# A graph network kernel: the steps behind the second pass's first four chunks come four to eight products later, and six constant writes move to product 20

## The chip, the cores and the metric

The kernel runs on one core of a Trainium2 chip. The metric is device microseconds of one execution, with the median of several runs. One execution was also taken by the hardware profiler; its rows are quoted below. PE is the engine of matrix products, PEld its weight loads, DVE the vector engine, ACT the scalar engine, POOL the general-purpose engine (here it issues gathers, transfers that fetch rows by a list of indices), SP the engine whose queue issues the plain loads.

## The reference

Four graph layers follow one another, each with a residual and a layernorm. `x` has 2708 rows of 128, `adj` is 2708 x 2708, all float32. The change is in the first layer and reaches into the second.

```python
def _L0_gnn_ref(x, A, W1, b1, W2, b2, sigma, k):          # sigma 1, k 4
    z = leaky_relu(_lap_mul(A, x) @ W1 + b1, 0.1)
    d2 = maximum(sq[:, None] + sq[None, :] - 2.0 * (z @ z.T), 0.0)
    S = exp(-sqrt(d2 + 1e-10) / (2.0 * sigma))
    S = where(ranks < k, S, 0.0)                          # the k largest of each row
    A2 = S + A
    return _lap_mul(A2, x) @ W2 + b2                      # d * (A2 @ (d * x))

def _L1_gnn_ref(X, A, W, a):
    XW = X @ W
    s_col, s_row = XW @ a[0, :f], XW @ a[0, f:]
    den = exp(leaky_relu(s_row[:, None] + s_col[None, :], 0.01))
    num = A @ den
    return A @ (where(num != 0, den / num, 0) @ XW)

x = layernorm(x + _L0_gnn_ref(...))
x = layernorm(x + _L1_gnn_ref(...))
...
```

## The kernel before, in words

**Tiles and chunks.** The 2708 rows are 22 tiles (T) of 128, the last one of 20 rows. The columns are cut into six chunks (C) of 512, 512, 512, 512, 384 and 276, that is of 4, 4, 4, 4, 3 and 3 tiles. A product of PE takes one tile of rows as weights and one chunk's columns of the adjacency matrix, and adds into an accumulator in PSUM (`acc`). One chunk takes 21 products, and every third chunk a few more for the tile of 20 rows.

**The second pass.** It forms A2 @ y2 of the first layer, y2 being the scaled x. `by_panels` (L189) runs over the chunks in order and, for each, over the row tiles; panels of four row tiles are loaded by SP into a ring of slots (L178). The part from S has four entries a row. The largest, the row itself, is a scaling by `own_sim` (L738), and three rows are gathered from memory by POOL (`gather_near` L727, L729) into one of nine buffers called `got`, and added by DVE with their weights (L742). `sum_near(t)` (L735) does this for one tile and leaves it in `near_sum`.

**What follows a chunk.** `end_pass2(c, acc)` (L974) is called behind a chunk's last product and registers these steps:

- `finish`: `add_near` (L744) adds the chunk's near sums to the accumulator by products with the identity (L749), and ACT copies it to `hT` (L981).
- `norm0`: the W2 product, one per tile (L789); DVE scales it and adds the residual (L794); then the layernorm: statistics on DVE (L272, L273), L255, the root on ACT (L242), its reciprocal (L243), the scaling (L277).
- `turn`: PE transposes the normalized tiles (L807), ACT copies them to `xT` (L810, three buffers).
- `find_c`: one product with the second layer's column vector (L861), ACT copies it to `c_row`, which is stored in hT's columns of that chunk (L862); DVE picks each row's own value (L866).
- `compare(t)`: DVE compares a tile's value with all values in `c_row` up to the tile (L893, L895; ties in L903) and writes a mask (four buffers). Its width grows with t.
- `times_w(c, t)`: XW of a tile (L874), copied by ACT to `xwe` (L875); `keep_xw(c)` writes the chunk's rows of it to memory, issued by POOL (L880).
- `rank_rows(t)`: ACT adds up a mask's rows (L911); `rank_columns(t)`: PE adds up its columns by t products one column wide (L916).

The last chunk has a path of its own (`n + 2` and later in `end_pass2`), which the diff doesn't touch. From it the ranks of the second layer's values are formed.

**The order.** PE, DVE and ACT run this stage in the order in which the program writes the instructions (`manual_schedule`, L1016). That order comes from the class `Due` (L31): `at(n, f, *args)` registers a step to be written when product n of the pass has been written, `tick` is called after each product and writes what is due; of two steps due at one product the one registered first comes first. So a step's number says behind how many products it stands on PE's queue, and equally where it stands on DVE's and ACT's among the other steps. The 132 products of the pass are numbered through. `sum_near(t)` is due at `near_at[t]` = 24 + 23 t // 5, so tile 0's at 24, tile 21's at 120. POOL's and SP's queues are ordered by the scheduler.

With n for the number of a chunk's `finish`, the chunks' numbers are n = 40, 59, 77, 96, 112 and 132. The W2 product comes at n + 2, the turn at n + 9, find_c at n + 11, compare of the chunk's k-th tile at n + 13 + 2k, times_w at n + 14 + 2k, rank_rows at n + 16 + 2k and rank_columns at n + 20 + 2k.

The W2 product, transposes, find_c and times_w share three small accumulators in PSUM (`mis`).

**The constants.** Ahead of the pass six DVE instructions fill `rk_f`, `fold` and `sel` (L774 to L781), which are first read behind the pass.

Of the kernel before, what the change touches and what calls it, by code (L numbers as in the profile page):

```python
# [22 lines left out]
CH = 4  # L23
MAGIC = 1.5 * 2**23
OOB = 4095
# [5 lines left out]
class Due:  # L31
# [5 lines left out]
    def at(self, n, f, *args):  # L37
        self.work.append((n, len(self.work), f, args))
        self.work.sort(key=lambda w: w[:2])
# [13 lines left out]
def kernel(  # L53
# [16 lines left out]
    nc = tc.nc  # L70
# [7 lines left out]
    C = len(starts)  # L78
# [5 lines left out]
    NCH = NB // CH  # L84
# [51 lines left out]
    ident = const.tile([P, P], F32, tag="ident", name="ident")  # L136
# [227 lines left out]
    with tc.tile_pool(name="knn", bufs=1) as knn:  # L364
# [97 lines left out]
        with (  # L462
# [5 lines left out]
            for c in range(C):  # L468
# [24 lines left out]
                ts = chunk_tiles[c]  # L493
# [180 lines left out]
        with tc.tile_pool(name="keys", bufs=3) as keys:  # L674

            for n, t in enumerate([*range(4, S), *range(4), *range(S, FULL)]):
                p = pw[t]
# [66 lines left out]
    def add_near(c, acc):  # L744
        ts = chunk_tiles[c]
        for t in ts:
            p = pw[t]
            o = t * P - starts[c]
            nc.tensor.matmul(  # L749
                acc[:, o : o + p], lhsT=near_sum[:p, t, :], rhs=ident[:p, :p], start=False, stop=(t == ts[-1])  # L750
            )
# [19 lines left out]
    spare = near.rearrange("p t k -> p (t k)")  # L771
    few_n, rk_f, neg_r = (spare[:, n * T : (n + 1) * T] for n in range(3))
    fold, sel = spare[:, 3 * T : 3 * T + 2 * NCH], spare[:, 3 * T + 2 * NCH : 3 * T + 2 * NCH + 2 * NB]
    nc.vector.memset(rk_f, float(OOB))  # L774
    nc.vector.tensor_add(fold, ident[:, : 2 * NCH], ident[:, 32 : 32 + 2 * NCH])
    for g in (64, 96):
        nc.vector.tensor_add(fold, fold, ident[:, g : g + 2 * NCH])
    nc.vector.memset(sel, 0.0)
    nc.vector.tensor_copy(
        sel.rearrange("p (a v) -> p a v", v=2 * CH)[:, :, :2], fold.rearrange("p (a v) -> p a v", v=2)  # L780
    )  # L781
    nc.vector.memset(rows_d, 0.0)
    add_bias(b2_sb)
    rk = rk_pool.tile([P, T], F32, tag="rk", name="rk")
# [181 lines left out]
    at = due.at  # L966
    near_at = [24 + (23 * t) // 5 for t in range(T)]
    for t in range(T):
        at(near_at[t], sum_near, t)

    ended = [-16]
    behind_last = []

    def end_pass2(c, acc):  # L974
        n = max(due.n + 1, near_at[chunk_tiles[c][-1]] + 3, ended[-1] + 16)
        ended.append(n)
        ts = chunk_tiles[c]

        def finish():
            add_near(c, acc)  # L980
            nc.scalar.copy(hT[:, cols[c]], acc[:, : cw[c]])  # L981

        at(n, finish)
        if c < C - 1:
            at(n + 2, norm0, ts)
            at(n + 9, turn, c)
            at(n + 11, find_c, c)
            for k, t in enumerate(ts):
                at(n + 13 + 2 * k, compare, t)
                at(n + 14 + 2 * k, times_w, c, t)  # L990
                if k == len(ts) - 1:
                    at(n + 14 + 2 * k, keep_xw, c)
                if c == C - 2 and k == len(ts) - 1:
                    behind_last.append(t)
                else:
                    at(n + 16 + 2 * k, rank_rows, t)
                if t:
                    at(n + (20 if c < C - 2 else 18) + 2 * k, rank_columns, t)
        else:
            for t in behind_last:  # L1000
                at(n + 1, rank_rows, t)
            at(n + 2, norm0, ts, True)
            at(n + 2, turn, c, True)
            at(n + 2, exp_table)
            at(n + 2, find_r)
            at(n + 3, last_stats)
            at(n + 3, last_rc)
            at(n + 3, turn_c, c)
            at(n + 3, negate_r)
            for k, t in enumerate(ts[:-1]):  # L1010
                at(n + 4 + k, compare, t)
                at(n + 4 + k, rank_rows, t)
                at(n + 5 + k, rank_columns, t)
            at(n + 3 + len(ts), compare_few)
            at(n + 4 + len(ts), exp_r)

    with tc.manual_schedule(engines={nc.tensor.engine, nc.vector.engine, nc.scalar.engine}):
        by_panels(
            rows_of(y2), end_pass2, due.tick, ready, [*range(S - 4), *range(S, T - 2), *range(S - 4, S), T - 2]
        )  # L1020
        due.flush()
# [23 lines left out]
    with tc.tile_pool(name="rank", bufs=1) as rank:  # L1045
# [326 lines left out]
        for c in range(C):  # L1372
            w = cw[c]
            begins = c % GROUPS == 0
            for i0 in range(0, FULL - 1, 4):
                if i0 < S:
                    n = c * G + i0 // 4
# [389 lines left out]
```

## Time and profile before

| what | value |
|---|---|
| runs of the kernel before | 1094.03, 1094.39, 1097.14 us; median 1094.39 us |
| the profiled execution | 1093.01 us, of which the span of the profile is 1091.3 us |
| PE, weight loads | busy 1000.2 us (92%), 482.7 us (44%) |
| DVE, ACT, POOL | busy 638.5 us (59%), 336.6 us (31%), 265.2 us (24%) |
| second pass | from 290 to 443 us of the span |
| gathers of near rows (L729) | 66 on POOL, 1.063 us each; POOL idle 37.5 us before them, most of it waiting for DVE's L742 |
| masks, sums of their rows | ACT's L911 takes 1.60 us for tile 12, 2.24 us for tile 18 |

The profile is one execution on the core. The page gives busy time and idle time of each engine, and what ended an idle time (the releaser, `<-`). "remote" or "another core or an unknown queue" stands where no instruction of this core's records explains the end of a wait, "issue" where the engine waited for nothing that is shown. In a timeline row the columns are the start, the duration, the engine, the line of the program, the operation, what is written from what, the shapes, how many instructions the row joins, and in square brackets the idle time before it with its releaser. In the row `PEclk` each digit is the clock that PE was granted in one of 40 slices, in tenths of full speed, a 9 being 0.9 or more.

### The profile page before, as it was taken

Reading aid. Unit: us, or ns where it says so; the run is one execution under the profiler, and the core shown is the slowest. Engines: PE = TensorE matmul, PEld = TensorE weight load, DVE = VectorE, ACT = ScalarE, POOL = GpSimd, SP = SyncE. Lnnn points to the kernel's source line nnn. Section 1 sums busy time; section 2 is a strip of 40 time slices with the busy share of each in tenths; the row PEclk is TensorE's granted clock in tenths of the full one; section 3 lists DMA queues with packets and bytes.
Section 4 is the critical chain, followed back from the end, with each engine's and each line's share of the span. In section 5 each row is a group of like instructions: output and inputs, shape, how many; then the busy total and the mean of one; then the engine's idle time right before and its main releaser. Section 6 shows DMA issues by size and latency. Waiting matters only on the chain.

```text
span 1091.3 us, 11487 instructions
## 1 busy us (share of the span) xinstructions
PE 1000.2 (92%) x3697; PEld 482.7 (44%) x3697; DVE 638.5 (59%) x1363; ACT 336.6 (31%) x617; POOL 265.2 (24%) x339
## 2 busy tenths in 40 slices
PE   0898999999987898798799999999999999999996
PEld 0445544444433455543233333334444644565444
DVE  5885448999934477772499999998112112132122
ACT  0000126555401144612467776665001100011000
POOL 4000000000575463015584344430112100000000
PEclk9889999999997899798899999999999999999998
DMA  9999340000383556497545545555775865574752
GB/s 341 357 329 276 102 137 1 0 1 1 100 279 89 186 160 205 141 369 228 136 131 153 154 122 166 143 143 181 230 232 157 275 229 183 170 238 158 240 158 77
DMA packets 109380, 190.31 MB, mean 174 GB/s; under 512 B 13666, under 2 KB 46706, under 8 KB 109310
## 3 DMA queue, kind: packets, MB, share of 16 engines
q1 hardware_dynamic: 91408, 151.79, 42.7%
q0 software_dynamic: 17728, 37.62, 12.5%
q8 instruction: 31, 0.51, 0.2%
q14 instruction: 39, 0.32, 0.1%
q10 hardware_dynamic: 174, 0.08, 0.0%
HBM read 214.37 MB, written 4.16 MB: 200 GB/s over the span
## 4 chain that ended last, share of the span: by engine, by line
PE 66%; DVE 16%; DMA 6%; issue 4%; ACT 3%; another core or an unknown queue 2%; POOL 2%; SPq 1%; POOLq 0%; DVEq 0%; ACTq 0%
PE acc L204 31%; PE num L1571 9%; PE hacc L1428 9%; PE acc L428 7%; DVE where L702 6%; DVE near L701 5%; DMA res<-in_adjT 3%; PE acc L1322 2%; PE mis L285 1%; PE acc L699 1%; DMA part<-in_adjT 1%; DMA got<-y_rows,where 1%; ACT junk L911 1%; DVE both L483 1%
## 5 line engine op out<-in xcount | busy, mean ns | idle before, releaser
L1449 POOL DMA_INDIRECT ring<-in_adjT,slot_i x88 | 95.4, 1084 | 117.7 <-PE num L1571 88.8
L1571 PE MATMUL num<-ring,lw 128*64 128x512 f32 (+1 forms) x528 | 115.6, 560 | 3.3 <-DVE err L1413 1.4
L1428 PE MATMUL hacc<-inv,xws 128*128 128x512 f32 (+1 forms) x264 | 111.7, 559 | 0.6 <-issue 0.3
L699 PE MATMUL acc<-zT,z 128*128 128x512 f32 (+2 forms) x252 | 102.2, 552 | 0.0
L1403 ACT ACTIVATE inv<-num,plain 128x1024 f32<-128x1024 f32 x88 | 80.6, 916 | 60.9 <-PE num L1571 38.6
L253 POOL TENSOR_TENSOR rstd<-rstd,minus_half 128x4 f32<-128x4 f32 (+1 forms) x18 | 17.3, 961 | 313.4 <-DVE rstd L252 313.4
L234 ACT COPY gb<-acc 128x512 f32<-128x512 f32 (+2 forms) x18 | 9.6, 535 | 251.1 <-PE acc L204 251.1
L1413 DVE TENSOR_TENSOR err<-inv,num 128x1024 f32<-128x1024 f32 x88 | 74.4, 854 | 20.4 <-ACT inv L1406 17.6
L700 ACT COPY key<-acc 128x512 f32<-128x512 f32 (+2 forms) x126 | 67.1, 535 | 55.1 <-issue 27.9
L204 PE MATMUL acc<-ring,y 128*128 128x512 f32 (+2 forms) x192 | 81.8, 556 | 0.5 <-issue 0.5
L1428 PEld LDWEIGHTS hacc<-inv,xws 128*128 128x128 f32 x264 | 46.5, 189 | 77.6 <-issue 45.2
L729 POOL DMA_INDIRECT got<-y_rows,where x66 | 70.2, 1063 | 37.5 <-DVE near_sum L742 18.9
L204 PE MATMUL acc<-ring,xs 128*128 128x512 f32 (+2 forms) x192 | 77.9, 549 | 0.0
L1420 DVE SCALAR_TENSOR_TENSOR inv<-gb,g_inv,inv 128x1024 f32<-128x1024 f32 x88 | 77.0, 913 | 0.1
L204 PE MATMUL acc<-ring,carry 128*128 128x512 f32 (+2 forms) x192 | 74.5, 542 | 0.0
L204 PE MATMUL acc<-ring,m_rows 128*128 128x512 f32 (+2 forms) x192 | 74.3, 542 | 0.0
L1417 DVE SCALAR_TENSOR_TENSOR inv<-err,inv 128x1024 f32<-128x1024 f32 x88 | 72.4, 861 | 0.1
L1406 ACT ACTIVATE inv<-inv 128x1024 f32<-128x1024 f32 x88 | 67.6, 768 | 2.8
L699 PEld LDWEIGHTS acc<-zT,z 128*128 128x128 f32 x252 | 45.8, 190 | 50.4 <-issue 45.0
L575 POOL TENSOR_TENSOR slot_e<-near,sim 128x44 f32<-128x44 f32 (+2 forms) x3 | 0.7, 245 | 269.7 <-DVE d2inv L603 267.6
L1571 PEld LDWEIGHTS num<-ring,lw 128*64 128x64 f32 x528 | 36.2, 138 | 65.0 <-issue 46.7
L701 DVE MAX8 near<-key 128x8 f32<-128x2708 f32 x21 | 62.2, 2964 | 2.7 <-ACT key L700 2.7
(378 smaller groups left out, 1392.0 us busy)
## 6 DMA issues: line engine op xcount, KB each, us to landing
ring<-in_adjT SPq DMA_DIRECT2D x86, 1024.0 KB
ring<-in_adjT SPq DMA_DIRECT2D x19, 768.0 KB
part<-in_adjT SPq DMA_DIRECT2D x12, 1024.0 KB
ring<-in_adjT SPq DMA_DIRECT2D x19, 552.0 KB
res<-in_adjT SPq DMA_DIRECT2D x4, 1280.0 KB
more<-in_adjT SPq DMA_DIRECT2D x4, 1024.0 KB
part<-in_adjT SPq DMA_DIRECT2D x3, 768.0 KB
part<-in_adjT SPq DMA_DIRECT2D x3, 552.0 KB
```

What stands on the lines that cost most here:

```text
L204: nc.tensor.matmul(accs[c][: lhsT.shape[-1], :w], lhsT=lhsT, rhs=src, start=start, stop=stop)
L428: nc.tensor.matmul(accs[c][:, : cw[c]], lhsT=y[:, i, :], rhs=src[:, : cw[c]], start=first, stop=last)
L699: nc.tensor.matmul(pks[c][:p, : cw[c]], lhsT=z2[:, :p], rhs=zT[:, cs], start=False, stop=True)
L701: nc.vector.max(near[:p, t, :], key[:p])
L729: nc.gpsimd.indirect_dma_start(out=got[:p, :], out_offset=None, in_=y2_rows[:, :], in_offset=bass.IndirectOffsetOnAxis(ap=where[:p, t, k : ...
L1403: nc.scalar.activation(inv, num[:, :w], AF.Ln, scale=plain[:, 0:1], bias=plain[:, 1:2])
L1413: nc.vector.tensor_mul(err, inv, num[:, :w])
L1417: nc.vector.scalar_tensor_tensor(inv, err, 2.0, inv, op0=ALU.subtract, op1=ALU.mult)
L1420: nc.vector.scalar_tensor_tensor(inv, gb[:, col : col + w], g_inv[:, q : q + 1], inv, op0=ALU.max, op1=ALU.mult)
L1428: nc.tensor.matmul(haccs[:, o:e], lhsT=xws[:, q, :], rhs=inv[:, o:e], start=(q == 0), stop=(q == NQ - 1))
L1449: nc.gpsimd.indirect_dma_start(out=rows[i][:KC, n, :], out_offset=None, in_=adj_half[:, :], in_offset=bass.IndirectOffsetOnAxis(ap=slot_i[ ...
L1571: nc.tensor.matmul(num[n * (BJ + 2) : (n + 1) * (BJ + 2), o:e], lhsT=lw[:, 2 * q + n, :], rhs=rows[i][:, n, c0 + o : c0 + e], start=True, ...
```

## The change

The six DVE instructions that fill `rk_f`, `fold` and `sel` become a function, registered for product 20 of the pass.

For chunks 0 to 3 (`c < C - 2`) `far` is 8, for chunk 4 it is 0. With it

- the W2 product with its layernorm moves from n + 2 to n + 6,
- the turn from n + 9 to n + 15,
- find_c from n + 11 to n + 19,
- compare, times_w, keep_xw, rank_rows and rank_columns each by eight products.

`finish` stays, so do all steps of chunks 4 and 5 and the near sums. The numbers of the W2 products are then 46, 65, 83, 102 and 114 (before 42, 61, 79, 98, 114), of the turns 55, 74, 92, 111 and 121 (before 49, 68, 86, 105, 121), of find_c 59, 78, 96, 115 and 123 (before 51, 70, 88, 107, 123).

```diff
-    nc.vector.memset(rk_f, float(OOB))
-    nc.vector.tensor_add(fold, ident[:, : 2 * NCH], ident[:, 32 : 32 + 2 * NCH])
-    for g in (64, 96):
-        nc.vector.tensor_add(fold, fold, ident[:, g : g + 2 * NCH])
-    nc.vector.memset(sel, 0.0)
-    nc.vector.tensor_copy(
-        sel.rearrange("p (a v) -> p a v", v=2 * CH)[:, :, :2], fold.rearrange("p (a v) -> p a v", v=2)
-    )
...
+    def set_constants():
...
+    at(20, set_constants)
...
         if c < C - 1:
-            at(n + 2, norm0, ts)
-            at(n + 9, turn, c)
-            at(n + 11, find_c, c)
+            far = (c < C - 2) * 8
+            at(n + (6 if far else 2), norm0, ts)
+            at(n + (15 if far else 9), turn, c)
+            at(n + (19 if far else 11), find_c, c)
             for k, t in enumerate(ts):
-                at(n + 13 + 2 * k, compare, t)
-                at(n + 14 + 2 * k, times_w, c, t)
+                at(n + far + 13 + 2 * k, compare, t)
+                at(n + far + 14 + 2 * k, times_w, c, t)
                 if k == len(ts) - 1:
-                    at(n + 14 + 2 * k, keep_xw, c)
+                    at(n + far + 14 + 2 * k, keep_xw, c)
                 if c == C - 2 and k == len(ts) - 1:
                     behind_last.append(t)
                 else:
-                    at(n + 16 + 2 * k, rank_rows, t)
+                    at(n + far + 16 + 2 * k, rank_rows, t)
                 if t:
-                    at(n + (20 if c < C - 2 else 18) + 2 * k, rank_columns, t)
+                    at(n + far + (20 if far else 18) + 2 * k, rank_columns, t)
```

The body of `set_constants` is the six instructions as they were.

More of the change, by code (lines that the diff above doesn't have):

```diff
@@ L969 @@
         at(near_at[t], sum_near, t)
+    def set_constants():
+        nc.vector.memset(rk_f, float(OOB))
+        nc.vector.tensor_add(fold, ident[:, : 2 * NCH], ident[:, 32 : 32 + 2 * NCH])
+        for g in (64, 96):
+            nc.vector.tensor_add(fold, fold, ident[:, g : g + 2 * NCH])
+        nc.vector.memset(sel, 0.0)
+        nc.vector.tensor_copy(
+            sel.rearrange("p (a v) -> p a v", v=2 * CH)[:, :, :2], fold.rearrange("p (a v) -> p a v", v=2)
+        )
+    at(20, set_constants)
     ended = [-16]
```

## The prediction

> **What bounds the kernel now.** I read first the busy shares in 40 slices, because they tell which engine fills the stage that the change touches. The second pass runs from 290 to 443 us of the span, slices 11 to 17 of 27.3 us each.
>
> ```profile
> PE   0898999999987898798799999999999999999996
> PEclk9889999999997899798899999999999999999998
> PE 66%; DVE 16%; DMA 6%; issue 4%; ACT 3%; another core or an unknown queue 2%; POOL 2%; SPq 1%; POOLq 0%; DVEq 0%; ACTq 0%
> ```
>
> PE is the bound in nearly every slice. The slices with 7 and 8 in the PE row carry a lower granted clock as well: here PE waits, and what follows a wait is slow. The third line is the chain of waits; its 2% without a known releaser matters below.
>
> Next the waits of 286 to 460 us (who waited, for whom; total, times, longest), for the gaps of PE and what DVE and ACT met at the same time.
>
> ```profile
> PE mis L807 <- DVE xs L277: 5.8, 1, 5.8
> PE acc L749 <- issue: 5.2, 1, 5.2
> PE mis L789 <- ACT hT L981: 4.9, 3, 3.7
> PE mis L861 <- issue: 2.0, 1, 2.0
> DVE xs L794 <- remote: 10.5, 1, 10.5
> ACT hT L981 <- remote: 2.7, 1, 2.7
> ```
>
> Two gaps belong to steps that move: 5.8 us where the turn (L807) waits for the normalized rows, 3.7 where the W2 product (L789) waits for hT. The 5.2 us before L749 wait for tile 3's gathers and don't move. Last the timeline (start, duration, idle before) tells why the rows were late.
>
> ```profile
> 332.84 1.25 PE L789 MATMUL mis<-w,hT 128*128 128x128 f32 x8
> 336.51 3.60 PE L204 MATMUL acc<-ring,y 128*128 128x512 f32 x8
> 345.90 1.24 PE L807 MATMUL mis<-ident,xs 128*128 128x128 f32 x4 [5.79 <-DVE xs L277]
> 346.93 3.57 PE L204 MATMUL acc<-ring,y 128*128 128x512 f32 x4
> ```
> ```profile
> 342.08 1.12 DVE L794 SCALAR_TENSOR_TENSOR xs<-mis,d2inv,xs 128x128 f32<-128x128 f32 x4 [10.47 <-remote]
> ```
> ```profile
> 338.46 1.01 POOL L729 DMA_INDIRECT got<-y_rows,where  x1 [0.30 <-issue]
> 347.46 1.01 POOL L729 DMA_INDIRECT got<-y_rows,where  x1 [7.99 <-DVE near_sum L742]
> ```
>
> Chunk 0's W2 ends at 332.84 + 1.25 = 334.1, yet DVE, idle since 331.6, starts on it only at 342.08, 8 us late; at most other places the consumer follows PE within 0.05 us. POOL issued gathers every 1.31 us until 339.47, and DVE started 2.6 us after that. I find the same at 363.1, the end of a run of 12 gathers (ACT's copy of chunk 1 starts at 364.76 for a product that ended at 359.79), and at 421.8, after 9. Runs of three to six gathers show none. My reading is that PE's completions reach the others late at the end of long runs of gathers, until the run ends. The mechanism is not shown.
>
> **The change part by part.** Base is the profiled execution, 1093.01 us (span 1091.3 and 1.7 around it); the median of the three runs is 1094.39, 1.4 above.
>
> Constants. Six DVE instructions leave the front of the pass for product 20. DVE runs in program order, and at product 20 nothing else has been written for it since; they stay between the last search and the first sums of gathered rows. Only L738's 0.2 us passes them: 0 to -0.2, I take -0.2.
>
> A, chunk 0's turn. W2 goes from product 42 to 46, the turn from 49 to 55, so six more products stand before the turn. A 512-wide product takes 0.86 us in unbroken stretches. PE's last product before the gap ended at 345.90 - 5.79 = 340.11; six more reach 345.26, and xs is ready at 345.84 if DVE still starts at 342.08. W2 then ends at 337.5, inside the late stretch as before, whose gathers don't move: DVE holds the same sums ahead of W2's result. Idle falls from 5.79 to 0.6: -5.15. After the old gap PE ran at half rate (transposes 1.24 against 0.60 at 412.95, four half products 3.57 against 1.88): 2.3 us that end too. Sum -7.45. If instead the delay of 8 us follows the product, DVE starts at 345.5 and the turn, due at 345.3, waits 4.0: then only -1.8. If no delay comes, all of 5.79 + 2.3 = -8.1.
>
> B, chunk 1's W2, product 61 to 65: four more products (3.44 us) in an idle of 3.67, and the half rate behind it (W2 2.08 against 1.05, the next product records 1.92 and 2.83 against 1.02 and 1.96: 2.8 us) may not come.
>
> ```profile
> 365.39 2.08 PE L789 MATMUL mis<-w,hT 128*128 128x128 f32 x8 [3.67 <-ACT hT L981]
> 387.74 1.05 PE L789 MATMUL mis<-w,hT 128*128 128x128 f32 x8
> ```
>
> Bounds -6.2 and 0. But sum_near(9) now precedes chunk 1's result on DVE, find_c and compare of chunk 0 sit later, and DVE frees the nine gather buffers earlier: the program puts 39 gathers ahead of the first keep_xw on POOL's queue, not 36. The run that begins at 347.5 can grow beyond 12, and a result can be late again. I take the middle, -3.2.
>
> C, chunk 2. Nothing waits there now: the W2 at 387.74 takes 1.05 at full clock. A new late stretch costs up to the worst gap seen, 5.8, and some half rate: bounds 0 and +6.5. Nearest are the runs of three to six gathers around it, with no delay: I take a quarter, +1.6.
>
> D, chunk 3's find_c goes from product 107 to 115, with it the idle of 2.01. The run of nine gathers whose end made it late stays and meets something else: 0 to -2.0, I take 0. E: its product (0.86) and one times_w (0.22) pass from ahead of chunk 4's finish to behind it: -1.1, if the end is set as below.
>
> F, the tail. Here the delay has no cover left. Chunk 4 keeps its distances, so chunk 3's eight-later work runs into it. In the trace ACT fills the end, with rank_rows one after another.
>
> ```profile
> 423.29 1.60 ACT L911 ACTIVATE junk<-mask 128x1664 bf16<-128x1664 bf16 x1
> 441.83 0.39 ACT L981 COPY hT<-acc 128x276 f32<-128x276 f32 x1
> ```
>
> Chunk 4's finish is at 421.08. Tile 12's rank_rows begins 2.2 us behind it, and the last hT copy ends 21.1 behind it (442.22). After the change chunk 4's W2 result (product 114) stands on DVE ahead of chunk 3's find_c (115) and masks (117 on): W2 ready 3.3 us after finish, norm0 3.6 (425.25 to 428.86), own 0.85, a sum_near 1.35, tile 12's mask 1.0: 10.1 us. From there ACT has six rank_rows with their reads (1.60 + 1.68 + 1.80 + 1.91 + 2.02 + 2.12 + 0.6 = 11.7), xT and a row copy (0.95), xwe copies (0.95) and hT's 0.39: 14.0. The last copy ends 24.1 behind finish, +3.0. Bounds: 0, if ACT interleaves as well as now, and +5.9, if all of the 7.9 later start but D's 2.0 stays.
>
> Sum: -0.2 - 7.45 - 3.2 + 1.6 + 0 - 1.1 + 3.0 = -7.35. Behind the pass the next stage waits on PE, DVE and ACT and not on a transfer, so a gain is kept. 1094.4 - 7.3 = 1087.0.
>
> A rule to weigh: the Trainium skill, "Perfetto Trace Analysis", "Optimization Strategy", says to find a gap, determine what blocks, and make the dependency start sooner or end faster. This change starts it later; by that rule each chunk would lose its four products, 3.44 us. The trace sides with the rule only in the tail, since in chunks 0 and 1 PE's time is what runs out.
>
> **The rivals.** R1, slower: new late stretches. For it: DVE frees buffers sooner, gather runs grow, and every run over eight had a late result at its end. Against: runs behind 365 had three to six gathers, DVE-bound. It decides when two of the results of chunks 1 to 3 are over 3.44 us late beyond what four products hide: each a gap and half rate of 6 us. -0.2 - 7.45 + 0 + 2 x 6 - 1.1 + 3.0 = +6.2, 1100.6.
>
> R2, no change: the delay follows the product. A gives -1.8, B 0, C 0, E -1.1, tail +3.0, constants -0.2: -0.1, 1094.3. For it: only one delay of 8 us was seen, and 334.1 + 8 fits as well as the end of the gathers. Against: the 2.6 us from the end of the run to the consumer come back as 1.6 and 0.9 at the two other places.
>
> R3, more: late results nowhere on PE's path. A -8.1, B -6.2, C 0, D -2.0, E -1.1, tail +3.0, constants -0.2: -14.6, 1079.8.
>
> That the change does nothing is true of the constants alone: 0.2 us at most.
>
> **How the numbers follow.** The forecast 1087.0 and its near neighbours 0.40, R3 and what lies towards it 0.16, R2 0.18, R1 0.26. Of a time, 0.3% (3.3 us) is about what a measurement of this kernel can tell from no change. The first two are faster: 0.56; R2 mostly within: 0.17; R1 and a little of R2 slower: 0.27. The forecast's own range is 1083 to 1091 (A's and B's bounds); the range of 8 in 10 takes in R3 and most of R1: 1079 to 1099.
>
> **What would show it.** A: chunk 0's turn with under 1 us idle before it, DVE's L794 twin still starting near 342, PE's clock at 1.0 from 340 to 362. B and C: idle before chunk 1's and 2's W2 and turn; a gap over 3 us speaks for R1, and then POOL's gathers must show a run over eight that ends 1 to 3 us before the late consumer. F: tile 12's rank_rows 10 us behind chunk 4's finish, the last hT copy 24 behind it. I am wrong if DVE starts on chunk 0's result about 8 us after W2's new end (R2), or if PE's gaps in the pass are no smaller in sum.

## The result, and the profile after

The changed kernel takes 1092.95 us (median of 11 runs, 1090.33 to 1098.79) against 1094.03 us before (11 runs, 1088.47 to 1097.14). The ratio is 0.9999 with an interval of 0.9977 to 1.0021: no change that the measurement can tell. The forecast was 1087.0 us and faster. The profiled execution has a span of 1091.3 us, the same as before.

Behind L774 the lines of the changed kernel are shifted: L794 is now L786, L789 is L781, L807 is L799, L911 is L903, L981 is L985, L916 is L908. First the page of the changed kernel: PE's busy tenths and granted clock.

```profile
PE   0898999999989897798699999999999999999996
PEclk9889999999999899698899999999999999999998
```

Slice 13 (327 to 355 us) rose from 7 to 9 in PE's row and in the clock's, but slice 14 still has 8 in both rows, slices 16 and 20 lost a tenth in PE's row and slice 17 one in the clock's. A gain came at one place and was given back at others. The waits of 286 to 460 us in the changed kernel (who, for whom; total, times, longest):

```profile
DVE xs L786 <- remote: 10.3, 1, 10.3
DVE xs L786 <- PE acc L204: 8.6, 1, 8.6
PE mis L799 <- DVE xs L277: 5.4, 2, 4.7
PE rk L908 <- issue: 2.9, 2, 2.2
```

DVE waits twice for a W2 result, 10.3 and 8.6 us. Before it stood idle for as long ahead of the same two results (10.5 and 9.3 us), but the second wait was for the product itself: DVE started 0.04 us behind W2's end (365.39 + 2.08 = 367.47).

```profile
367.51 1.13 DVE L794 SCALAR_TENSOR_TENSOR xs<-mis,d2inv,xs 128x128 f32<-128x128 f32 x4 [9.27 <-PE mis L789]
```

PE's gap ahead of a turn was 5.8 us, in one piece; it is 0.7 and 4.7. The timelines of the changed kernel show which chunk has which (start, duration, idle before):

```profile
336.29 1.05 PE L781 MATMUL mis<-w,hT 128*128 128x128 f32 x8
337.18 7.89 PE L204 MATMUL acc<-ring,y 128*128 128x512 f32 x18
345.78 1.09 PE L799 MATMUL mis<-ident,xs 128*128 128x128 f32 x4 [0.71 <-DVE xs L277]
...
357.50 1.05 PE L781 MATMUL mis<-w,hT 128*128 128x128 f32 x8
...
372.66 1.24 PE L799 MATMUL mis<-ident,xs 128*128 128x128 f32 x4 [4.70 <-DVE xs L277]
```
```profile
341.97 1.12 DVE L786 SCALAR_TENSOR_TENSOR xs<-mis,d2inv,xs 128x128 f32<-128x128 f32 x4 [10.33 <-remote]
...
368.85 0.35 DVE L786 SCALAR_TENSOR_TENSOR xs<-mis,d2inv,xs 128x128 f32<-128x128 f32 x1 [8.64 <-PE acc L204]
```
```profile
338.08 1.01 POOL L729 DMA_INDIRECT got<-y_rows,where  x1 [0.30 <-issue]
347.35 1.01 POOL L729 DMA_INDIRECT got<-y_rows,where  x1 [8.26 <-DVE near_sum L742]
...
366.05 1.01 POOL L729 DMA_INDIRECT got<-y_rows,where  x1 [0.31 <-issue]
```

Chunk 0 went as worked out: its result is taken at 341.97 (before 342.08), and the turn stands at 345.78 with six more products done, 0.71 us idle before it. Chunk 1's W2 ends at 358.55, but DVE starts on it at 368.85, 10.3 us later. POOL's gathers ran without a break from 347.35 to 367.06, 15 of them where there were 12, and DVE started 1.8 us behind the last.

The account, from the end of each chunk's finish (L749), before and after: chunk 1 359.8 and 352.1 (-7.7); chunk 2 386.0 and 379.2 (-6.8); chunk 3 404.9 and 397.7 (-7.2); chunk 4 421.9 and 416.1 (-5.8); the last hT copy starts at 441.8 and 438.7 (-3.1). So 7.7 us were won up to chunk 1's finish; 0.9 went from chunk 1's finish to chunk 2's, 0.4 came back up to chunk 3's, 1.4 went up to chunk 4's and 2.7 in the tail. The last 3.1 went behind the pass. There the product that finds the slots (`sl`) ended 2.6 us earlier (495.9 against 498.5), and DVE took it up at the same time as before (498.6):

```profile
494.55 1.36 PE L1174 MATMUL sl<-val_b,hot_in 128*128 128x132 f32 x8
```
```profile
498.40 0.31 DVE L1290 TENSOR_SCALAR slot_i<-sl 128x44 uint32<-128x44 f32 x2 [7.19 <-PE mis L1063]
```

That is one more result taken 2.5 us late, inside a run of 14 gathers of the next layer (487.8 to 506.5). From the start of the last hT copy to the next stage's first product took 88.2 us before and 91.1 after.

### The profile page after: what moved, and what is told of

Same layout as the page of the kernel before. It is cut to its first block, busy times and chain, and to the rows that moved or that the text cites. A ratio compares the mean times of both kernels' runs of the same rounds, so it can differ in the third digit from the quotient of the medians.

```text
span 1091.3 us, 11489 instructions
## 1 busy us (share of the span) xinstructions
PE 1003.4 (92%) x3697; PEld 484.9 (44%) x3697; DVE 638.2 (58%) x1363; ACT 336.4 (31%) x617; POOL 266.0 (24%) x339
## 4 chain that ended last, share of the span: by engine, by line
PE 64%; DVE 16%; issue 7%; DMA 5%; POOL 4%; ACT 2%; another core or an unknown queue 1%; SPq 0%; POOLq 0%; DVEq 0%; ACTq 0%
PE acc L204 31%; PE hacc L1433 8%; PE num L1576 8%; PE acc L428 7%; DVE where L702 6%; DVE near L701 5%; DMA res<-in_adjT 3%; POOL xws L1044 1%; PE acc L1327 1%; PE mis L285 1%; POOL ring L1454 1%; PE acc L699 1%; DMA part<-in_adjT 1%; DVE both L483 1%
```

## The experiments

The runs come in sets; the kernels of one set ran on one chip, with the kernel before timed beside them, and the sets came to different chips. They are named by the kernel before's median there: B (1094.66 us), C (1061.05 in one set, 1061.16 in another), D (1089.66), E (1091.15). Ratios are to the kernel before of the same set. The kernel before was profiled only on D and on the chip of the result above ("the first chip"), whose number is not on record: it may be one of B, D and E.

**Fewer buffers for gathered rows (B).** The reading behind the forecast was that PE's completions arrive late while POOL issues gathers without a break. In the profile before, DVE had added 15 gathers when it stood still, and POOL stopped at 24 = 15 + 9 buffers; after the change at 39 = 30 + 9. So a second half was added: the wait lasts until POOL has used up its buffers, because DVE frees none.

```diff
-    got_pool = late.enter_context(tc.tile_pool(name="got", bufs=9, side="right"))
+    got_pool = late.enter_context(tc.tile_pool(name="got", bufs=6, side="right"))
```

> The kernel before, with 6 buffers for gathered rows in place of 9. Theory T (PE's completions are held back while POOL issues gathers without a break, and DVE, which waits for such a completion, frees no buffer, so that the delay lasts until POOL has used up its buffers): POOL runs out 3 gathers (3.9 us) sooner, chunk 0's W2 result is taken by DVE at 338 instead of 342.1, PE's gap before the turn shrinks from 5.8 to about 2 us, chunk 1's hT copy starts some 4 us sooner; the pass ends 6 to 10 us earlier, the time falls by 4 to 10. Rival W (the results are late in these stretches whatever POOL does): both starts stay within 1 us of 342.1 and 364.8, time unchanged within 2. Rival G (fewer buffers slow the gathers): finishes wait for near_sum, slower by 2 or more.

> The kernel before, with 4 buffers. Theory T: POOL runs out 5 gathers (6.6 us) sooner, chunk 0's W2 result is taken at 335.5, the turn does not wait; the pass ends 10 to 14 us earlier if the gathers keep pace (first landing takes 4.6 us from its issue, so four buffers give one gather per 1.2 to 1.5 us). Rival W: no change of the starts. Rival G: slower by 2 or more through finishes that wait for near_sum.

Six buffers: ratio 0.9973 (0.9958 to 0.9989); four: 0.9926 (0.9910 to 0.9942). The timelines, POOL and DVE of the kernel with six:

```profile
332.84 1.01 POOL L729 DMA_INDIRECT got<-y_rows,where  x1 [0.30 <-issue]
341.71 1.01 POOL L729 DMA_INDIRECT got<-y_rows,where  x1 [7.86 <-DVE near_sum L742]
```
```profile
336.32 1.13 DVE L794 SCALAR_TENSOR_TENSOR xs<-mis,d2inv,xs 128x128 f32<-128x128 f32 x4 [7.63 <-remote]
```

and PE and DVE of the one with four:

```profile
331.11 1.05 PE L789 MATMUL mis<-w,hT 128*128 128x128 f32 x8
338.01 0.60 PE L807 MATMUL mis<-ident,xs 128*128 128x128 f32 x4
```
```profile
332.20 1.13 DVE L794 SCALAR_TENSOR_TENSOR xs<-mis,d2inv,xs 128x128 f32<-128x128 f32 x4 [3.57 <-PE mis L789]
```

With six, POOL stops 3 gathers earlier, and DVE starts 4.3 us behind W2's end (332.0), on the first chip with nine 8.0; 2.5 us behind the last gather's end, there 2.6. With four, the longest run ahead of W2 has eight gathers, and the result is taken within 0.1 us; the turn has no gap. Rival W falls for four buffers. For six this profile does not decide: with nine buffers the kernel before was only 4.9 us late on D (below), and the median fell by 3.1 us where 4 to 10 were expected. With four the pass takes 126.8 us from the first gather to the last hT copy; the kernel before took 133.8 on the first chip and 128.7 on D, so the expected 10 to 14 us are not shown. The time fell by 9.4 us.

**Parts of the change (B).**

```diff
-            far = (c < C - 2) * 8
+            far = (c < 1) * 8
...
-                    at(n + far + (20 if far else 18) + 2 * k, rank_columns, t)
+                    at(n + far + (20 if c < C - 2 else 18) + 2 * k, rank_columns, t)
```

and `c < 2` for chunks 0 and 1, `c < 3` for chunks 0 to 2.

> The changed kernel with the later places for chunk 0 alone (chunks 1 to 3 as before). Theory T: finish of chunk 1 comes 7.7 us earlier as in the changed kernel; DVE halts behind tile 8 and POOL after 36 gathers at 363, so chunk 1's normalized rows come at 368.6 and its turn, nine products behind W2, waits some 7 us; the pass ends 3 to 4 us before that of the kernel before, without the late tail: time about 1 to 3 below before. Rival (what the change loses is lost only in chunk 3's tail): chunk 1 does not wait longer than before and the pass ends 8 us earlier.

> The changed kernel with the later places for chunks 0 and 1 alone. Theory T: chunk 1's turn waits 4.7 us as in the changed kernel; the tail behind chunk 4's finish is back to 21 us from 24; the pass ends 5 to 6 us before that of the kernel before, time 2 to 5 below. Rival (delays of chunks 2 and 3 are what brings the rest): no better than the changed kernel, within 1 us of before.

Chunk 0 alone: 0.9937 (0.9914 to 0.9960). Chunks 0 and 1: 0.9925 (0.9909 to 0.9941), that is 1086.09 us. Parts of the change bring what the whole, on the first chip, did not. The two medians (1085.83 and 1086.09 us) differ by 0.3: chunk 1's later places add nothing to chunk 0's, although the forecast gave them 3.2. In the profile of chunks 0 and 1 chunk 1's result is again late, by 9.6 us, and its turn waits 5.0. With chunk 0 alone the turn did not wait 7 us, as expected, but 2.2: its result came 4.2 us late, not 10. That was a miss; a late result has no fixed size.

**The same kernel elsewhere (C).**

> The changed kernel itself once more, on the same chip as the next three. Theory T (the late completions last until POOL's run of gathers ends, and runs end where DVE halts): the order of DVE's work is fixed, so the runs of 24, 15, 6, 6, 12 and 3 gathers come again and chunk 1's result is taken again about 10 us late, its turn waits 4 to 5 us. Time 1091 to 1095, 5 to 8 above the kernel with the later places for chunks 0 and 1 alone (1086.1). Rival (the first profile caught a rare arrangement): other runs, other waits, and a time nearer 1086.

> The changed kernel with the later places for chunks 0 to 2, chunk 3 as before. If chunk 3's delay is what the changed kernel loses (a run of 12 gathers behind 395, results 2 us late, gaps of 2.2 and 0.7 us ahead of its turn, rank rows of tile 12 begin 9 us behind chunk 4's finish): about 1086, like chunks 0 and 1 alone. If chunk 2's delay is: about 1092, like the changed kernel.

Here the kernel before takes 1061.05 us, 33 less than on the first chip; both expectations had reckoned with a time near 1094. The changed kernel is 0.31% slower (1.0031, 1.0012 to 1.0051), chunks 0 to 2 alone 1.0019 (0.9996 to 1.0041). POOL, DVE and PE of the changed kernel on this chip:

```profile
337.53 1.01 POOL L729 DMA_INDIRECT got<-y_rows,where  x1 [0.31 <-DVE st L272]
341.36 1.01 POOL L729 DMA_INDIRECT got<-y_rows,where  x1 [2.82 <-DVE near_sum L742]
```
```profile
335.97 1.13 DVE L786 SCALAR_TENSOR_TENSOR xs<-mis,d2inv,xs 128x128 f32<-128x128 f32 x4 [6.36 <-PE mis L781]
355.81 1.13 DVE L786 SCALAR_TENSOR_TENSOR xs<-mis,d2inv,xs 128x128 f32<-128x128 f32 x4 [1.07 <-PE mis L781]
```
```profile
334.88 1.05 PE L781 MATMUL mis<-w,hT 128*128 128x128 f32 x8
343.50 0.60 PE L799 MATMUL mis<-ident,xs 128*128 128x128 f32 x4
354.72 1.05 PE L781 MATMUL mis<-w,hT 128*128 128x128 f32 x8
364.03 0.60 PE L799 MATMUL mis<-ident,xs 128*128 128x128 f32 x4
```

The runs of gathers are the same, 24 and 15 at 1.31 us each, but the first two W2 results are taken 0.04 us behind W2's end (335.93 and 355.77), DVE works while POOL is still issuing, and both turns run at full rate without a gap. So unbroken gathers are not enough to make a result late; it depends on the chip too. The two profiles of the changed kernel differ by 28.6 us in span: 13.4 up to the last hT copy, 14.3 from there to the next stage's first product (91.1 against 76.8), and 0.9 in all the rest. The two stretches are those with gathers in long runs.

**Four buffers with the later places (C).**

> The changed kernel with 4 buffers for gathered rows in place of 9. Theory T: no run of more than some nine gathers, chunk 1's result at most 4 us late instead of 10, its turn without a wait; the pass ends 4 to 8 us before that of the changed kernel, of which a part is lost behind the pass: 1084 to 1089. Rival W (late whatever POOL does): chunk 1's result 10 us late again, 1092 to 1094.

> Later places for chunks 0 and 1 alone, and 4 buffers. Theory T: both cures remove the same waits, so the gains do not add: like the kernel before with 4 buffers (1085.2) within 3 us, 1082 to 1088. If they were independent, 1094.7 - 8 - 9 = 1077.

1.0211 (1.0186 to 1.0237) and 1.0166 (1.0141 to 1.0192): slower by 23.7 and 18.6 us, both expectations missed. Rival G, that fewer buffers slow the gathers, decides here. The waits of 300 to 450 us with four buffers, and of 300 to 430 us in the changed kernel on the same chip:

```profile
DVE near_sum L742 <- DMA got<-y_rows,where: 46.9, 23, 4.8
...
PE acc L749 <- DVE near_sum L742: 13.4, 3, 6.2
```
```profile
DVE near_sum L742 <- DMA got<-y_rows,where: 16.2, 8, 4.8
```

DVE waits 46.9 us for gathers that were issued too late for want of a buffer, and PE's finishes wait for DVE; the last gather ends at 433.9 instead of 405.9. So nine buffers have their use where results are on time. (On this chip four were tried with the later places only.)

**Without the gathers (D, then C).** `c01_again` repeats chunks 0 and 1, `before_again` gives a second profile of the kernel before. Two kernels leave out the fetching of near rows, so they compute something else, and only their waits are of use:

```diff
-            got = got_pool.tile([P, D], F32, tag="got", name="got")
-            gather_near(got, t, TOPK + k)
-            nc.vector.scalar_tensor_tensor(g, got[:p], sim[:p, t, k : k + 1], g, op0=ALU.mult, op1=ALU.add)
+            nc.vector.scalar_tensor_tensor(g, y2[:p, t, :], sim[:p, t, k : k + 1], g, op0=ALU.mult, op1=ALU.add)
```

and, in a kernel that keeps a transfer of the same size, `nc.gpsimd.dma_start(out=got[:p, :], in_=y2_rows[t * P : t * P + p, :])` in place of the gather.

> The kernel before once more, for a second profile. If the runs behind this one come from a chip where it takes about 1094: chunk 0's W2 result is taken some 8 us late, gathers in runs of 24, 12, 6, 6, 6, 3 and 9. If it takes about 1061: the results are taken within 0.2 us in the same stretches, chunk 0's turn waits at most 1 us, and the last hT copy comes some 23 to 25 us earlier than on the first chip.

> Later places for chunks 0 and 1 alone, once more beside before. Where completions are late (before about 1094): 0.5 to 1.0% faster as in the first run of it. Where they are not (before about 1061), theory T gives nothing to hide: the same as before within 0.3%; the rival, that the gaps which these two delays fill exist on every chip, gives 0.5% faster there too.

> The kernel before, with each gather of near rows replaced by a plain transfer of the same size issued by POOL into the same nine buffers (the rows fetched are a tile's own, not the near ones). Where completions are late: if POOL's unbroken issuing of any transfer holds PE's completions back, chunk 0's result is again 6 to 9 us late; if it takes the indirect gathers, it is on time (within 0.3 us) and the pass ends 10 to 20 us earlier. Where they are not late it can't tell.

> The kernel before without the gathers of near rows (DVE adds a tile's own rows with the same weights instead). Where completions are late: theory T says that every late result of the pass goes with the gathers, chunk 0's result within 0.3 us of W2's end, and the pass ends 15 to 25 us earlier; the later stage's late weights (fetches of 14 rows behind 485) stay. Rival W (results are late on that chip whatever POOL does): still 4 us or more late.

Before again: 0.9983 (0.9949 to 1.0017). Chunks 0 and 1: 0.9940 (0.9914 to 0.9965). One run each gave 1077.54 us with plain transfers and 1072.63 without. DVE's start on chunk 0's result, first in the kernel before (W2 ends at 331.9), then without gathers (W2 ends at 327.4):

```profile
336.80 1.13 DVE L794 SCALAR_TENSOR_TENSOR xs<-mis,d2inv,xs 128x128 f32<-128x128 f32 x4 [6.90 <-issue]
```
```profile
327.43 1.13 DVE L792 SCALAR_TENSOR_TENSOR xs<-mis,d2inv,xs 128x128 f32<-128x128 f32 x4 [15.59 <-PE mis L787]
```

4.9 us late on this chip with the gathers, on time without them, and the last hT copy starts at 419.5 instead of 435.1. The stretch from the last hT copy to the next stage's first product, which keeps 14 gathers of its own, still took 88.5 us. Here DVE started 1.1 us ahead of the end of the last gather (337.9), so "until the run is over" is not exact. With plain transfers the results are on time too, but that does not show that it takes indirect ones: a plain transfer took POOL some 0.55 us, so POOL ran out of buffers by 318 us and issued nothing while W2 ran. That question stays open.

> The changed kernel beside the next three. Where completions are late (before at 1088 or more): the same as before within 0.3%, turn of chunk 1 waits 3 to 5 us. Where they are not (before about 1061): 0.2 to 0.5% slower, as in its second run.

> Later places for chunks 0 to 2, chunk 3 as before. If chunk 3's delay takes the gain back (work of chunk 3 behind chunk 4's finish, late results of a run of 12 gathers): 0.5 to 0.8% faster than before where completions are late. If chunk 2's does: within 0.3% of before.

> Before without the gathers of near rows, timed. Theory T: 12 to 20 us below before where completions are late; 0 to 4 below where they are not.

> The changed kernel without the gathers of near rows. Theory T (the change gains only where a result is late, and costs its tail always): no PE gap ahead of a turn or W2 product is there to fill, chunk 4's finish to the last hT copy takes 2 to 3 us longer than in before without gathers; 0 to 4 us slower than it. Rival (the change gains by itself, as the gaps are there without gathers too): 3 us or more faster than before without gathers.

This set ran on C again. The changed kernel: 1.0052 (1.0028 to 1.0077); chunks 0 to 2: 1.0035 (1.0021 to 1.0049); without gathers, before: 0.9942 (0.9922 to 0.9962), after: 0.9968 (0.9941 to 0.9996). The last two are 1054.53 and 1056.77 us, so by itself the change costs about 2.2 us, though the intervals overlap. Without gathers the kernel before reaches its last hT copy at 418.0 us here and at 419.5 on D; the two chips differ by 1.4 us up to there, and by 12.2 (76.3 against 88.5) in the stretch behind it. With the gathers the changed kernel's two chips differed by 13.4 us up to there, so in the pass the difference goes with the gathers, as far as one profile each can tell. The place of the 2.2 us is ACT's end of the pass, without gathers, first before and then after:

```profile
397.81 0.48 ACT L979 COPY hT<-acc 128x384 f32<-128x384 f32 x1 [1.51 <-PE acc L747]
398.19 1.59 ACT L909 ACTIVATE junk<-mask 128x1664 bf16<-128x1664 bf16 x1
...
418.04 0.41 ACT L979 COPY hT<-acc 128x276 f32<-128x276 f32 x1
```
```profile
398.80 0.48 ACT L983 COPY hT<-acc 128x384 f32<-128x384 f32 x1 [0.16 <-PE acc L747]
...
407.31 1.59 ACT L901 ACTIVATE junk<-mask 128x1664 bf16<-128x1664 bf16 x1 [3.70 <-DVE mask L883]
...
422.01 0.40 ACT L983 COPY hT<-acc 128x276 f32<-128x276 f32 x1
```

From chunk 4's hT copy to the last one 20.2 us before, 23.2 after. Tile 12's rank rows begin 0.4 us behind the copy's start before and 8.5 after, for want of a mask.

**Chunk 3 (E).**

> Later places for chunks 0 to 2. Where completions are late (before at 1088 or more): if chunk 3's delay is what takes the gain back, 0.5 to 0.8% faster, as chunks 0 and 1 alone; if chunk 2's is, within 0.3% of before and behind chunks 0 and 1 alone. Where they are on time (before about 1061): 0.2 to 0.4% slower, as in its two runs there.

> Later places for chunks 0 and 1 alone. Where completions are late: 0.6 to 0.8% faster, as in its two runs. Where they are on time: there is no late result to hide and chunks 2 and 3 keep their places in front of chunk 4's finish, so within 0.3% of before; if the two delays cost by themselves, slower by over 0.3%.

Chunks 0 to 2: 0.9934 (0.9910 to 0.9959), 1084.58 us; chunks 0 and 1: 0.9908 (0.9873 to 0.9942), 1082.15 us. Chunk 2's delay does not take the gain back. Since the whole change gave 0.9999, chunk 3's is left; but the whole change was not timed beside these, so this compares two sets, and it is not shown that chunk 3's delay alone takes some 7 us. The traces give part of it: from chunk 4's finish to the last hT copy 20.3 us here, 22.6 with chunk 3 moved on the first chip.

The later places for chunks 0 and 1 alone beat the kernel before on B, D and E, by 0.6 to 0.9%; the changed kernel was not timed in these sets. With nine buffers they weren't timed on C, where chunks 0 to 2 are 0.2 to 0.35% slower.

## Why the prediction was wrong, step by step

- **Where PE waits, and why** held in part: gaps stand behind results that are taken late near long runs of gathers, and without the gathers on D the late results and the gaps are gone. "At the end of long runs, until the run ends" was too simple: it depends on the chip, and on D the result came before the run's end. The first profile had a row against it as well: chunk 3's turn ended at 412.95 + 0.60 = 413.55, ACT took it 2.7 us late, and that was inside the run of nine (409.7 to 421.8), 5.6 us before its end (row below). PE's clock was read too broadly also: of the slices of the pass with 7 or 8 in PE's row, 13, 14 and 17 have a lower clock, but 12 and 16 have 9.

```profile
416.21 0.59 ACT L810 COPY xT<-mis 128x512 f32<-128x512 f32 x1 [3.62 <-PE acc L204]
```

- **A** held in this profile: forecast -7.45, measured -7.7 at chunk 1's finish, DVE at 341.97, 0.71 us idle. The near agreement is partly luck: 0.3 of the 7.7 stand ahead of the first gather, and 0.7 are three products of times_w (0.22 each) that now come behind this finish. The size also hangs on how late the result is: on D, where it was 4.9 us late and the turn had waited 2.7, chunk 1's finish came 2.9 us earlier (47.6 us behind the first gather before, 44.7 with the later places). On C the changed kernel has no gap here; the kernel before has no profile there.
- **B** is the step that failed first. The middle of 0 and -6.2 was taken (-3.2); chunk 1's finish to chunk 2's lost 0.9. The text had named the reason, that sum_near(9) now stands ahead of chunk 1's result, DVE frees buffers for longer, and the run grows: from 12 to 15 gathers. W2 ran without a gap, as forecast, but its result was taken 10.3 us late, and the turn, nine products behind it, waited 4.7 us, with the half rate behind it (1.24 us for the transposes). So the gap moved from W2 to the turn. Chunk 1's result was late with the later places in each such profile on B, D and E too (5.9 to 9.6 us), and on B these places brought nothing (1086.09 against 1085.83 us). The middle of two bounds was a choice against the text's own argument.
- **C**: forecast +1.6, measured -0.4 from chunk 2's finish to chunk 3's. R1's further stretches came once, not twice.
- **D and E**: forecast -1.1 together, measured +1.4 from chunk 3's finish to chunk 4's. Overlooked was DVE's order: chunk 2's last masks, eight products later, now stand behind chunk 3's W2 result, which DVE took 2.3 us behind W2's end (403.78). PE's column sums of tile 10 wait 2.18 us for their mask; the 0.70 us inside them has no releaser in the profile. The old idle of 2.0 us at find_c is gone, 2.9 us have come. And E counted the work that leaves this stretch, not what chunk 2 brings in: four products of times_w stand here where there were two.

```profile
406.08 1.12 DVE L786 SCALAR_TENSOR_TENSOR xs<-mis,d2inv,xs 128x128 f32<-128x128 f32 x4 [1.12 <-PE mis L866]
...
410.53 0.95 DVE L885 TENSOR_SCALAR mask<-hT,cc 128x1408 bf16<-128x1408 f32 x1
```
```profile
411.53 0.35 PE L908 MATMUL rk<-ones_b,mask 128*128 128x1 bf16 x8 [2.18 <-issue]
412.58 0.19 PE L908 MATMUL rk<-ones_b,mask 128*128 128x1 bf16 x2 [0.70 <-issue]
```

Chunk 3's W2 and tile 10's compare are both due at product 102. Of two steps due at one product it is not always the one registered first that comes first, as is said above of `Due`: `at` breaks the tie by the number of steps that wait at that moment (`len(self.work)`), which falls as steps are written. By the rows W2's result comes ahead of the mask, which was registered first.

- **F** held: forecast +3.0, measured +2.7, and +3.0 without gathers on C. Tile 12's rank rows start 9.8 us behind chunk 4's finish (10.1 forecast), the last copy ends 23.8 behind it (24.1).

```profile
425.05 1.59 ACT L903 ACTIVATE junk<-mask 128x1664 bf16<-128x1664 bf16 x1 [3.71 <-DVE mask L885]
...
438.68 0.40 ACT L985 COPY hT<-acc 128x276 f32<-128x276 f32 x1
```

- **"A gain is kept behind the pass"** failed in the profiled execution: the 3.1 us left were lost there, 3.0 of them by the time DVE took the slots (498.40 against 498.55). On the chips with late results this stretch took 86.5 to 92.4 us in twelve profiles, with no order that follows the pass, so a single profile can't show a gain or a loss of 3 us there.
- **Constants**: nothing was seen of them, and no run moved them alone.
- **The rivals.** R2's time came, 1094.3 against 1092.95, but not its mechanism: DVE did not start 8 us behind W2's new end. R1's mechanism took part of the gain. R3's condition (nothing late) is what the changed kernel meets on C, with the other sign: 0.3 to 0.5% of cost. R3 credited the change with gaps that, as far as the kernels without gathers show, are not there when nothing is late.

The sum, forecast and measured: constants -0.2 and unseen, A -7.45 and -7.7, B -3.2 and +0.9, C +1.6 and -0.4, D and E -1.1 and +1.4, F +3.0 and +2.7, behind the pass 0 and +3.1: -7.35 and 0.0.

## What to carry to other kernels

When a result is taken long after its product ended, ask what releases it before asking how much work would cover the wait: moving the product later does not help if something else sets that time, while moving its consumer (here the turn) does. A fixed delay for every chunk piles up on the last ones, whose cover is gone; give it to the first chunks only, where the gap was measured. And a gap of a few us that the profile puts down to an unknown queue may be a property of the chip: time the change on more than one before building on it, and keep in mind that the recording may have a part in it (below).

## What the runs showed of the hardware that was not expected

The kernel before takes 1061 us on one chip (twice) and 1090 to 1095 on others. The changed kernel's two profiles have the same pace of gathers (1.31 us) and nearly the same time everywhere but in two stretches. In those, results of PE are taken up to 10 us late on the slower chips; on the fast one DVE takes the first two within 0.1 us of W2's end.

It is PE's signal that comes late, not DVE's start: in the first profile the semaphore that PE raises (the counter DVE waits on) changed at 329.65, 342.06 and 342.20 us for products that ended at 329.64, 334.10 and 340.11, and DVE started at 342.08. In the same stretches the recording itself is incomplete. From 290 to 440 us the kept traces hold 1015 records of semaphore changes for the kernel before on the first chip and 1049 on D, but 2126 on D with plain transfers, where nothing was late, and 2083 for the changed kernel on C; without the gathers it is 1078 on D and 1088 on C. Late signals and lost records come together. Each execution here has a recorded span and clock, so no run shows whether the signals would be late without the recording: that rival is open. PE itself shows small gaps in the later stretch: in the changed kernel on the first chip seven of 0.27 to 0.83 us from 501 to 509 us, where it waits for nothing that the profile shows. Why the chips differ was not found.
